# Ten early units, other store queues and other load times in the convolution tail of a two-layer image kernel

## Chip, cores and metric

The kernel runs on one core of one Trainium2 chip, in float32. The metric is the device time of one execution in microseconds (us); the median of several runs counts. The five engines are TensorE (PE), VectorE (DVE), ScalarE (ACT), GpSimd (POOL) and SyncE (SP). Each follows its own list of instructions in order; DMA transfers are issued by SP, POOL or ACT from the same lists.

## What is computed

Two layers over x of shape (2, 256, 64, 64): two images, 256 channels, 64 x 64 pixels. Layer 0 is a full attention over 4096 pixels with eight heads, blended with x by a mask. Layer 1 is a gated window attention followed by two grouped 7 x 7 convolutions, whose result gates the rows again. Cut to that:

```python
# layer 0
q = proj(Wq, bq) / sqrt(hd); k = proj(Wk, bk); v = proj(Wv, bv)
attn = softmax(einsum('bnd,bmd->bnm', q, k))            # 4096 x 4096, 16 times
hybrid = conv1x1(concat([x, attn @ v]), Wf, bf)
x = hybrid * m + x * (1 - m)
# layer 1
x = x * sigmoid(relu(x @ ca_w1 + ca_b1) @ ca_w2 + ca_b2)
x = x + window_attention(x)                             # windows of 8 x 8, four heads
x = shuffle(x)                                          # channels (4, 64) -> (64, 4)
y = relu(bn1(conv7x7(x, sa_w1, groups=64)))             # 256 -> 64 channels
y = bn2(conv7x7(y, sa_w2, groups=64))                   # 64 -> 256 channels
return x * sigmoid(y)
```

## The kernel before

**Order of the whole.** Projections come first (to about 190 us). Then a loop runs over `slots`: image b, chunk c of 512 queries, half g of the heads, block m of 128 keys. After the last block of a chunk, its denominators are computed (line 690), spread through DRAM (`inv_s`, then `rd`), and a generator `stage` (line 731) does layer 1 up to the convolutions for these 512 pixels, eight image rows. The stages of all chunks but the last run between the attention's products, a piece at a time. The stage of the last chunk of image 1 runs after the loop (lines 1227 to 1234), alternating with pieces of the convolution. Its own pieces on TensorE are, in order: hya (fuse; second half needs fa, which waits for rd), ca1, ca2, qka (twice), sca, vwa, pta, oa, opa. At its end the sum x + o is written to `xo` by VectorE (line 974) and stored to DRAM in `x_s` (line 989), in three overlapping blocks of rows. All loads of rows for the convolution read `x_s`, so those of image 1 need the last of these stores.

**The convolution.** 64 groups are taken four at a time: a unit u (16 of them, `NU`) has 16 channels. An item is a unit with image 0, with image 1 or with both; `items` (line 998) is the order in which they run. Before: units 0 to 7 of image 0, units 2 to 7 of image 1, units 8 to 15 of both, and units 1 and 0 of image 1: 24 items. Since the first eight (`EARLY`) need image 0 alone, they can run beside the last stage. For item k:

- `load_x(k)` reads its rows, 420 KB an image, into one of four buffers (`xea` for the first EARLY items, `xla` for the others, number k % 4). So the rows of item k+4 go where those of item k were.
- `load_w(u)` reads the unit's banded weights, 896 KB, into a rotating pool of eight (unit 0 has its own buffer; unit 1 is read a second time at the end).
- `conv1` (TensorE, line 1057): 28 products into one PSUM tile, of which there is one; ScalarE evicts it with Relu into `yca` (line 1065).
- `conv2` (line 1082): 56 products into two PSUM pairs; ScalarE evicts with Tanh (line 1093) and a scaling Copy (line 1099) into `z`. The trace shows each product twice.
- `gate` (line 1110): VectorE multiplies z by the rows; then 12 stores an image, 24 or 16 KB each, go to the output.

On TensorE the order is c1(k+1), c2(k), c1(k+2), c2(k+1) and so on: c1(k) and c2(k) below are conv1 and conv2 of item k. `convolve` is a generator with a yield after every conv1 and every conv2, so the gate of item k, the loads behind it and conv1 of item k+2 are written out as one piece.

**What sets the order.** The schedule is manual: each engine's list is the order in which the program writes instructions. An SP load written behind stores waits until these could be issued, and they wait for their z. Before:

- Stores alternate between POOL and SP; while `staged` is true (the last stage has ended) and k < EARLY, between POOL and ACT; for the last two items between ACT and SP. Stores on ACT are `held` and issued after the next item's evictions (line 1101).
- Behind the gate of item k the rows of item k+4 are loaded (`load_rows(k + 4)`, line 1167); at the end of the stage, four loads at once (line 1144).
- Weights: four loads ahead (units 1 to 4, line 1151), then one behind each gate: units 5 to 9 at once, units 10 and on from item 8.
- The last chunk's `x_s` stores: two on SP and two on POOL (line 988).
- Two pieces of the convolution run in the wait for the denominators (line 1230).

Of the kernel before, what the change touches and what calls it, by code (L numbers as in the profile page):

```python
# [12 lines left out]
AF = mybir.ActivationFunctionType  # L13
# [4 lines left out]
B, C, H, W = 2, 256, 64, 64  # L18
# [4 lines left out]
NCHUNK = N // CH  # L23
# [6 lines left out]
AHEAD = 2  # L30
EB = 8
DN = 8
EARLY = 8
HEADS1, HD1 = 4, 64
WS = 8
NW = W // WS
# [9 lines left out]
UG = 4  # L46
UQ = UG // 4
NU = NG // UG
# [9 lines left out]
def conv_seq_kernel(ctx: ExitStack, tc: tile.TileContext, a, out):  # L58
    nc = tc.nc
# [463 lines left out]
    def pipeline(arm, shifted, pools):  # L523
# [207 lines left out]
        def stage(b, c):  # L731
# [241 lines left out]
            for oc in range(KC):  # L973
                nc.vector.tensor_add(  # L974
                    xo[:, oc, :, PAD : PAD + W].rearrange("p r (w c) -> p w r c", c=WS),
                    y[:, oc, :].rearrange("p (w r c) -> p w r c", w=NW, r=WS),
                    u[:, oc, :].rearrange("p (w r c) -> p w r c", w=NW, r=WS),
                )
                for n, (x0, _, _) in enumerate(BLOCKS):

                    r0, r1 = max(WS * c, x0 - 1), min(WS * c + WS, x0 + 31)
                    if r0 >= r1:
                        continue
                    for h in range(2):
                        q = 2 * oc + h
                        p = 32 * q + 1 - x0

                        eng = nc.sync if h == 1 and (b, c) == (B - 1, NCHUNK - 1) else nc.gpsimd
                        eng.dma_start(  # L989
                            x_s[b, n, p + r0 : p + r1].rearrange("r g w -> g r w"),  # L990
                            xo[64 * h : 64 * h + 64, oc, r0 - WS * c : r1 - WS * c, :],
                        )
# [9 lines left out]
        def convolve():  # L1002
# [8 lines left out]
            for k in range(2):  # L1011
                t = cpool.tile([P, B * nb, WP], F32, name=f"yc{arm}{k}")
                nc.gpsimd.memset(t, 0.0)
                ycs.append(t)
            xs, ws, ys = {}, {}, {}

            weights = deque([*range(1, NU), 1])
            dst = out.rearrange("b (g i) r w -> b i r g w", i=4)
# [53 lines left out]
            def conv2(k):  # L1072
                u, images = items[k]
                n = nb * len(images)
                y = ys.pop(k)
                w = ws[u][:, 32 * UW :].rearrange("p (m d) -> p d m", d=KS)
                tiles = [psum2(f"c2{arm}{k}_{hh}") for hh in range(2)]
                for d in range(KS):
                    for j in range(4):
                        r = slice(32 * j, 32 * j + 32)  # L1080
                        for o in HALVES:
                            nc.tensor.matmul(  # L1082
                                tiles[j // 2][o, j % 2, 0 : n * W],
                                w[r, d, o],
                                y[r, 0:n, d : d + W],
                                start=(d == 0),
                                stop=(d == KS - 1),
                            )
                zs = []
                for m in range(len(images)):  # L1090
                    z = pool.tile([P, 4, nb * W], F32, tag="z", name=f"z{arm}{k}_{m}", bufs=4)
                    for hh in range(2):
                        nc.scalar.activation(  # L1093
                            z[:, 2 * hh : 2 * hh + 2, :],
                            tiles[hh][:, :, m * nb * W : (m + 1) * nb * W],
                            AF.Tanh,
                            scale=0.5,
                        )
                    nc.scalar.activation(z, z, AF.Copy, bias=0.25, scale=0.25)  # L1099
                    zs.append(z.rearrange("p j (n x) -> p j n x", x=W))  # L1100
                while held:
                    held.popleft()()
                return zs

            def gate(k, zs):
                u, images = items[k]
                for m, b in enumerate(images):
                    z = zs[m]
                    x = xs[k][:, nb * m : nb * m + nb, :, PAD : PAD + W]
                    nc.vector.tensor_mul(z, z, x.rearrange("p n g x -> p g n x"))  # L1110

                    engines = (nc.gpsimd, nc.sync)
                    if k >= len(items) - 2:
                        engines = (nc.scalar, nc.sync)
                    elif staged and k < EARLY:
                        engines = (nc.gpsimd, nc.scalar)
                    stores = 0
                    for n, (x0, r0, r1) in enumerate(BLOCKS):
                        for i in range(4):
                            p = 32 * i + 1 - x0  # L1120
                            stores += 1
                            args = (
                                dst[b, i, r0:r1, UG * u : UG * u + UG, :],
                                z[p + r0 : p + r1, :, n, :],
                            )
                            eng = engines[stores % len(engines)]
                            if eng is nc.scalar:
                                held.append(lambda a=args: nc.scalar.dma_start(*a))
                            else:
                                eng.dma_start(*args)  # L1130
                if k == len(items) - 1:
                    while held:
                        held.popleft()()


            def more():
                if staged and not xcs:

                    for n in range(3):
                        t = ep.tile([P, HG, CH], F32, tag="sum", name=f"xl{arm}{n}", bufs=3)  # L1140
                        t = t.rearrange("p h n -> p (h n)")[:, 0 : B * nb * UG * WP]
                        xcs.append(t.rearrange("p (n g w) -> p n g w", n=B * nb, g=UG, w=WP))
                    xcs.append(pool.tile([P, B * nb, UG, WP], F32, name=f"xl{arm}3"))
                    load_rows(EARLY + 3)
                return bool(xcs)


            load_rows(3)
            load_w(0)
            pool = yield  # L1150
            for _ in range(4):
                load_w(weights.popleft())
            conv1(0)
            yield
            for k, (u, images) in enumerate(items):
                while len(xs) <= k + 1 < len(items):
                    if not more():
                        yield
                conv1(k + 1)
                yield  # L1160
                more()
                z = conv2(k)
                yield
                more()
                gate(k, z)
                if xcs or k + 4 < EARLY:
                    load_rows(k + 4)

                if weights and (weights[0] <= 1 + EB or k >= EARLY):
                    load_w(weights.popleft())  # L1170

        def run_later():
# [150 lines left out]
```

## Time and profile before

| quantity | value |
|---|---|
| three runs | 2920.15, 2926.58, 2927.13 us; median 2926.58 |
| profiled execution | 2921.04 us, of it span 2919.3 us |
| mean granted TensorE clock | 0.996 |
| busy in the span | PE 2881.9, PEld 837.2, DVE 2434.9, ACT 2455.9, POOL 315.1 us |
| last attention product | ends at about 2700.6 us |
| last stage on TensorE | 2713.0 (hya) to 2763.2 us (opa) |
| conv1 and conv2 busy | 2700.2 to 2905.0 us |
| c1 products | 448 on xea, 896 on xla |
| stores of the output | 180 on POOL, 168 on SP, 36 on ACT |
| DMA in 2700 to 2920 us | 33.92 MB, mean 154 GB/s |

Times within the span count from its start. A line of the timeline gives the start, the length, engine and source line, operation, what is written and read, shape and number of instructions, and in brackets how long the engine had been idle and what ended that. PE is a matmul, PEld a weight load into the array; SPq, ACTq and POOLq are the lists that issue DMAs, and the length there is that of issuing, not of the transfer. The tail of the span, from 2700 us, is the part that the change touches.

### The profile page before, as it was taken

Reading aid. Unit: us, or ns where it says so; the run is one execution under the profiler, and the core shown is the slowest. Engines: PE = TensorE matmul, PEld = TensorE weight load, DVE = VectorE, ACT = ScalarE, POOL = GpSimd, SP = SyncE. Lnnn points to the kernel's source line nnn. Section 1 sums busy time; section 2 is a strip of 40 time slices with the busy share of each in tenths; the row PEclk is TensorE's granted clock in tenths of the full one; section 3 lists DMA queues with packets and bytes.
Section 4 is the critical chain, followed back from the end, with each engine's and each line's share of the span. In section 5 each row is a group of like instructions: output and inputs, shape, how many; then the busy total and the mean of one; then the engine's idle time right before and its main releaser. Section 6 shows DMA issues by size and latency. Waiting matters only on the chain.

```text
span 2919.3 us, 85528 instructions
## 1 busy us (share of the span) xinstructions
PE 2881.9 (99%) x37322; PEld 837.2 (29%) x37322; DVE 2434.9 (83%) x1356; ACT 2455.9 (84%) x4143; POOL 315.1 (11%) x560
## 2 busy tenths in 40 slices
PE   9999999999999999999999999999999999999998
PEld 3551222222222222222222222222222222222665
DVE  3339999899999898998989999989899899999211
ACT  5569989898989898988989898989899898989433
POOL 8010000000000101010000000000101010000356
PEclk9999999999999999999999999999999999999999
DMA  8545422222232323242222223222324232232474
GB/s 245 202 172 174 134 75 63 78 68 80 56 88 65 90 61 91 65 80 71 70 75 69 79 55 82 64 83 63 77 73 84 70 73 75 69 113 88 117 228 120
DMA packets 231124, 276.26 MB, mean 95 GB/s; under 512 B 118672, under 2 KB 135252, under 8 KB 230484
## 3 DMA queue, kind: packets, MB, share of 16 engines
q1 hardware_dynamic: 200996, 231.74, 27.3%
q0 software_dynamic: 22416, 35.61, 5.5%
q8 instruction: 295, 4.83, 0.7%
q10 hardware_dynamic: 7328, 3.36, 0.4%
q14 instruction: 89, 0.73, 0.1%
HBM read 221.88 MB, written 66.39 MB: 99 GB/s over the span
## 4 chain that ended last, share of the span: by engine, by line
PE 97%; DMA 1%; ACT 1%; DVE 0%; issue 0%; SPq 0%; POOL 0%; ACTq 0%; DVEq 0%; POOLq 0%
PE sa L633 37%; PE ava L669 35%; PE hya L519 4%; PE qka L519 4%; PE c2a L1082 2%; PE q L428 2%; PE c1a L1057 2%; PE opa L519 2%; PE vwa L519 2%; PE v L465 2%; PE k L428 2%; PE dna L695 1%; PE sca L847 1%; PE pta L922 1%; PE oa L941 1%; PE ca2a L785 1%
## 5 line engine op out<-in xcount | busy, mean ns | idle before, releaser
L646 ACT ACTIVATE ea<-sa 128x512 f32<-128x512 f32 (+1 forms) x3072 | 2036.7, 746 | 51.6 <-PE sa L633 26.6
L633 PE MATMUL sa<-qa,ka 32*64 32x512 f32 x16384 | 1145.9, 613 | 1.5 <-ACT vst L473 1.2
L675 DVE TENSOR_TENSOR suma<-suma,ea 128x2048 f32<-128x2048 f32 x480 | 1097.4, 2286 | 5.7 <-ACT ea L646 0.5
L669 PE MATMUL ava<-ea,va 128*32 128x512 f32 x8192 | 1091.1, 605 | 1.0
L675 DVE TENSOR_TENSOR odda<-odda,ea 128x2048 f32<-128x2048 f32 x420 | 959.4, 2284 | 50.6 <-ACT ea L646 50.6
L633 PEld LDWEIGHTS sa<-qa,ka 32*64 32x64 f32 x16384 | 241.7, 129 | 785.4 <-ACT ea L646 713.6
L669 PEld LDWEIGHTS ava<-ea,va 128*32 128x32 f32 x8192 | 161.5, 108 | 834.1 <-issue 804.6
L989 POOL DMA_DIRECT2D xs<-xo x94 | 66.6, 716 | 1761.8 <-DVE xo L974 1758.8
L675 DVE TENSOR_TENSOR suma<-ea,ea 128x2048 f32<-128x2048 f32 x32 | 73.2, 2287 | 58.8 <-ACT ea L646 58.8
L519 PE MATMUL qka<-ua,qkv_w 128*32 128x512 f32 x1024 | 115.8, 592 | 0.3 <-DVE ua L803 0.3
L1130 POOL DMA_DIRECT2D out_dram<-za x180 | 101.3, 571 | 77.8 <-DVE za L1110 56.3
L447 DVE TENSOR_REDUCE top<-sq 128x512 f32<-128x2048 f32 x16 | 36.6, 2286 | 81.6 <-ACT sq L441 81.6
L750 ACT ACTIVATE ta<-hya,bf 128x512 f32<-128x512 f32 x32 | 20.2, 683 | 97.3 <-PE hya L519 91.3
L1110 DVE TENSOR_TENSOR za<-za,xla 128x768 f32<-128x768 f32 x24 | 23.0, 960 | 94.3 <-ACT za L1099 53.7
L707 POOL DMA_DIRECT2D invs<-inva x62 | 34.1, 558 | 599.2 <-DVE inva L721 438.9
L754 DVE TENSOR_TENSOR ta<-ta,mca 128x512 f32<-128x512 f32 x32 | 22.0, 688 | 77.4 <-ACT ta L750 77.4
L868 ACT ACTIVATE ewa<-ewa,mxwa 128x64 f32<-128x64 f32 x256 | 85.3, 346 | 1.5 <-DVE mxwa L859 1.5
L1082 PE MATMUL c2a<-yca,wa 32*64 32x192 f32 (+1 forms) x2688 | 83.7, 387 | 2.6 <-issue 2.3
L1093 ACT ACTIVATE za<-c2a 128x384 f32<-128x384 f32 x64 | 27.8, 486 | 57.9 <-PE c2a L1082 41.6
L826 ACT ACTIVATE qka<-qka,qkv_b 128x512 f32<-128x512 f32 x64 | 40.3, 681 | 40.8 <-PE qka L519 40.8
L1082 PEld LDWEIGHTS c2a<-yca,wa 32*64 32x64 f32 x2688 | 64.7, 192 | 22.0 <-issue 12.7
L677 DVE TENSOR_TENSOR suma<-suma,odda 128x2048 f32<-128x2048 f32 x30 | 68.8, 2292 | 1.0
(138 smaller groups left out, 1675.9 us busy)
## 6 DMA issues: line engine op xcount, KB each, us to landing
ka<-ks SPq DMA_DIRECT2D x256, 256.0 KB
va<-vs SPq DMA_DIRECT2D x256, 256.0 KB
wa<-ws SPq DMA_DIRECT2D x17, 896.0 KB
ws<-zeros SPq DMA_DIRECT2D x16, 896.0 KB
xs<-xo POOLq DMA_DIRECT2D x78, 140.0 KB, 6.0
xla<-xs SPq DMA_DIRECT2D x24, 420.0 KB
x<-in_x_dram SPq DMA_DIRECT2D x16, 512.0 KB
qs<-qst SPq DMA_DIRECT2D x16, 512.0 KB
```

What stands on the lines that cost most here:

```text
L428: nc.tensor.matmul(s[:, g, :], w[:, kc, g * P : (g + 1) * P], rhs, start=(kc == 0), stop=(kc == KC - 1),)
L465: nc.tensor.matmul(sv[:, m, :], xs0[i][:, kc, m * P : (m + 1) * P], wv[:, kc, :], start=(kc == 0), stop=(kc == KC - 1),)
L519: nc.tensor.matmul(out[o : o + 32], weights[:, o : o + 32], x, start=start, stop=stop)
L633: nc.tensor.matmul(heads[j][o], k[r, cols][:, o], q[r, g, :], start=True, stop=not shifted)
L646: nc.scalar.activation(e[:, h, :], tile, AF.Exp, scale=SCALE0)
L669: nc.tensor.matmul(av[r, :], v[:, m % PB, r], e[:, j, :], start=start, stop=stop)
L675: nc.vector.tensor_add(total, first.pop(m % chains, total), e)
L677: nc.vector.tensor_add(acc[1], acc[1], acc[2])
L868: nc.scalar.activation(e[:, n, :], e[:, n, :], AF.Exp, bias=mx[:, n : n + 1], accum_out=rs[:, n : n + 1],)
L989: eng.dma_start(x_s[b, n, p + r0 : p + r1].rearrange("r g w -> g r w"), xo[64 * h : 64 * h + 64, oc, r0 - WS * c : r1 - WS * c, :],)
L1082: nc.tensor.matmul(tiles[j // 2][o, j % 2, 0 : n * W], w[r, d, o], y[r, 0:n, d : d + W], start=(d == 0), stop=(d == KS - 1),)
L1130: eng.dma_start(*args)
```

## The change

- `EARLY` is 10: units 0 to 9 of image 0 run by themselves, then units 2 to 9 of image 1, units 10 to 15 of both, and units 1 and 0 of image 1: 26 items.
- Stores of an item go to POOL alone until `staged`, then to POOL and SP in turn. Nothing is held on ACT but half the stores of the last item.
- The last item's z is evicted, gated and stored by blocks of 64 columns (three of them) instead of whole.
- All four `x_s` stores of the last chunk go to SP.
- Two weight loads go ahead instead of four. Behind the gate of item k, unit u is loaded once `due(u)` is at most k: units 3 and 4 behind item 1, units 5 to 9 behind items 2 to 6, units 10 to 15 behind items 15 to 20, unit 1 again behind item 21.
- Rows of items below EARLY are loaded behind item k-4 as before; those of the others, k+3 behind item k's stores, one item at a time, and not four at once.
- One more piece of the convolution, c2(1), runs ahead of the last stage's hya.

The order that results on TensorE around the last stage is: c1(0), c1(1), denominators, c2(0), c1(2), c2(1), hya, c1(3), ca1, ca2, c2(2), qka, c1(4), sca, qka, c2(3), sca, vwa, c1(5), pta, c2(4), oa, c1(6), opa, c2(5), c1(7), c2(6), c1(8). Before it was: c1(0), c1(1), denominators, c2(0), c1(2), hya, c2(1), ca1, ca2, c1(3), qka, c2(2), sca, qka, c1(4), sca, vwa, c2(3), pta, c1(5), oa, c2(4), opa, c1(6), c2(5), c1(7), c2(6), c1(8).

```diff
-EARLY = 8
+EARLY = 10
...
-                        eng = nc.sync if h == 1 and (b, c) == (B - 1, NCHUNK - 1) else nc.gpsimd
+                        eng = nc.gpsimd
+                        if (b, c) == (B - 1, NCHUNK - 1):
+                            eng = nc.sync
...
+            at_unit = [0]
...
+                    if k < len(items) - 1:
+                        evict(z, tiles, slice(m * nb * W, (m + 1) * nb * W))
                     zs.append(z.rearrange("p j (n x) -> p j n x", x=W))
-                while held:
-                    held.popleft()()
-                return zs
+                return zs, tiles
...
+            def store(k, b, n, z, engines):
+                u = items[k][0]
+                x0, r0, r1 = BLOCKS[n]
+                for i in range(4):
+                    p = 32 * i + 1 - x0
+                    eng = engines[(4 * n + i) % len(engines)]
...
+            def gate(k, zs, tiles):
+                for m, b in enumerate(items[k][1]):
...
+                    if k == len(items) - 1:
+                        for n in range(nb):
+                            evict(z[:, :, n, :], tiles, slice(n * W, (n + 1) * W))
+                            nc.vector.tensor_mul(z[:, :, n, :], z[:, :, n, :], x[:, :, n, :])
+                            store(k, b, n, z, (nc.sync, nc.scalar))
+                        while held:
+                            held.popleft()()
+                        continue
+                    nc.vector.tensor_mul(z, z, x)
+                    engines = (nc.gpsimd,)
+                    if staged:
+                        engines = (nc.gpsimd, nc.sync)
+                    for n in range(nb):
+                        store(k, b, n, z, engines)
...
+            def due(u):
+                if u < EARLY:
+                    return max(1, u - 3) if len(ws) < NU else len(items) - 5
+                return u + EARLY - 5
...
-                    load_rows(EARLY + 3)
+                if xcs:
+                    load_rows(min(len(xs), at_unit[0] + 2))
                 return bool(xcs)
...
-            for _ in range(4):
+            for _ in range(2):
                 load_w(weights.popleft())
...
-                gate(k, z)
-                if xcs or k + 4 < EARLY:
+                gate(k, *z)
+                at_unit[0] = k + 1
+                if k + 4 < EARLY:
                     load_rows(k + 4)
-
-                if weights and (weights[0] <= 1 + EB or k >= EARLY):
+                more()
+
+                while weights and due(weights[0]) <= k:
                     load_w(weights.popleft())
...
-            if now[0] in (len(slots) + DN, len(slots) + DN + 1):
+            if len(slots) + DN <= now[0] <= len(slots) + DN + 2:
                 next(conv)
```

More of the change, by code (lines that the diff above doesn't have):

```diff
@@ L1091, in conv2 @@
                     z = pool.tile([P, 4, nb * W], F32, tag="z", name=f"z{arm}{k}_{m}", bufs=4)
[L1092 to L1099, printed above, removed]
@@ L1100, in conv2 @@
-                    zs.append(z.rearrange("p j (n x) -> p j n x", x=W))
-                while held:
-                    held.popleft()()
-                return zs
-            def gate(k, zs):
-                u, images = items[k]
-                for m, b in enumerate(images):
+                    if k < len(items) - 1:
+                        evict(z, tiles, slice(m * nb * W, (m + 1) * nb * W))
+                    zs.append(z.rearrange("p j (n x) -> p j n x", x=W))
+                return zs, tiles
@@ new lines, in evict @@
+            def evict(z, tiles, cols):
+                for hh in range(2):
+                    nc.scalar.activation(
+                        z[:, 2 * hh : 2 * hh + 2, :],
+                        tiles[hh][:, :, cols],
+                        AF.Tanh,
+                        scale=0.5,
+                    )
+                nc.scalar.activation(z, z, AF.Copy, bias=0.25, scale=0.25)
+            def store(k, b, n, z, engines):
[4 more added lines that the diff above has]
+                    eng = engines[(4 * n + i) % len(engines)]
+                    args = (
+                        dst[b, i, r0:r1, UG * u : UG * u + UG, :],
+                        z[p + r0 : p + r1, :, n, :],
+                    )
+                    if eng is nc.scalar:
+                        held.append(lambda a=args: nc.scalar.dma_start(*a))
+                    else:
+                        eng.dma_start(*args)
@@ L1108, in gate @@
+            def gate(k, zs, tiles):
+                for m, b in enumerate(items[k][1]):
                     z = zs[m]
                     x = xs[k][:, nb * m : nb * m + nb, :, PAD : PAD + W]
[L1110 to L1130, printed above, removed]
@@ L1131, in gate @@
-                if k == len(items) - 1:
-                    while held:
-                        held.popleft()()
+                    x = x.rearrange("p n g x -> p g n x")
+                    if k == len(items) - 1:
[6 more added lines that the diff above has]
+                        continue
```

## The prediction

> **What bounds the kernel now.** I read the share of the chain by engine, then the timeline behind the last attention product, the granted clock by microsecond, and the queue of SyncE. An item is a unit of 16 channels for one image or for both; c1(k) and c2(k) are the two convolutions of item k on TensorE, and e(k) is the end of c2(k).
>
> ```profile
> PE 97%; DMA 1%; ACT 1%; DVE 0%; issue 0%; SPq 0%; POOL 0%; ACTq 0%; DVEq 0%; POOLq 0%
> ```
>
> The chain is TensorE nearly throughout. The diff leaves everything before 2700 us alone, so only the last 219 us of the span can move, and there it matters when TensorE waits. The timeline just after the last stage (its last projection ends at 2762.9, counted to the modelled end of its work):
>
> ```profile
> 2764.65 1.39 SPq L989 DMA_DIRECT2D xs<-xo  x2
> ...
> 2769.01 11.08 ACTq L1128 DMA_DIRECT2D out_dram<-za  x6
> ...
> 2772.76 2.90 SPq L1036 DMA_DIRECT2D xla<-xs  x4
> 2772.76 3.76 PE L1082 MATMUL c2a<-yca,wa 32*64 32x192 f32 x107 [1.73 <-issue]
> ...
> 2780.14 0.42 ACT L1065 ACTIVATE yca<-c1a,cbias 128x192 f32<-128x192 f32 x1 [10.34 <-DMA xla<-xs]
> ...
> 2780.61 4.26 PE L1057 MATMUL c1a<-xla,wa 128*32 128x192 f32 x56 [4.09 <-ACT yca L1065]
> ```
>
> Here TensorE runs dry: image 1 must be stored and read back, and six held stores sit on ScalarE's queue for 11.08 us ahead of the eviction that c1(8) needs. Idle 1.73 + 4.09 us; two convolutions also run slowly, 3.76 and 4.26 us. Why, the stretches of 1 us show (columns: length, PE, PEld, DVE, ACT, POOL, granted clock, DMA share, GB/s):
>
> ```profile
> 2773.00:2774.00 1.00, 1.00 (x57) 1.00 (x57) 0.00 (x0) 0.00 (x0) 1.00 (x3) 1.00 0.31 43
> 2774.00:2775.00 1.00, 1.00 (x42) 1.00 (x35) 0.00 (x0) 0.00 (x0) 1.00 (x3) 0.51 0.78 226
> ...
> 2783.00:2784.00 1.00, 1.00 (x20) 0.62 (x16) 0.19 (x1) 0.00 (x0) 0.51 (x1) 0.50 0.04 7
> 2784.00:2785.00 1.00, 1.00 (x28) 0.55 (x27) 0.00 (x0) 0.00 (x0) 1.00 (x3) 0.87 0.34 73
> ```
>
> The granted clock halves at 2774.0, although TensorE is busy again and had idled only 1.73 us, and comes back at 2784.2. Beyond that TensorE is dense. One item there:
>
> ```profile
> 2789.83 2.64 PE L1082 MATMUL c2a<-yca,wa 32*64 32x192 f32 x112
> ...
> 2794.26 0.96 DVE L1110 TENSOR_TENSOR za<-za,xla 128x768 f32<-128x768 f32 x1 [4.07 <-ACT za L1099]
> ...
> 2795.24 2.54 SPq L1130 DMA_DIRECT2D out_dram<-za  x6
> ...
> 2797.45 2.53 PE L1057 MATMUL c1a<-xla,wa 128*32 128x192 f32 x56
> ...
> 2797.90 0.39 SPq L1036 DMA_DIRECT2D xla<-xs  x1
> ```
>
> c2(8) ends at 2792.47. Its gate ends at 2795.22, its six SyncE stores are issued by 2797.78, and only then, 5.43 us after e(8), goes the load of rows: those of item 12, whose c1 starts at 2802.48. The next two items give 5.29 and 5.33; I take 5.35. Between lies c1(11), at 2797.45, before the load is issued.
>
> **The work itself.** Convolution steps start 2.47 (c1) and 2.57 us (c2) apart for one image, 4.73 and 4.80 for two: 5.04 and 9.53 an item. Splitting units 8 and 9 costs 2 x (10.08 - 9.53) = +1.1. By the changed order c1(6) moves ahead of the last projection, -2.5 behind it; c2(1) in turn fills the 1.68 us in which TensorE waits for fa, and the stage after it swaps equals (c1 for c2), so I put no change there. Unhindered, after the projection: 7.61 (c2(5), c1(7), c2(6)) + 10.08 (to e(8)) + 110.15 (c1(10) to c2(25)) = 127.84 us, ending at 2890.7. Now it ends at 2905.0: **-14.3**, the gain of filling the gap with image 0.
>
> **The stage: weights of unit 3 come late.** Four weight loads go out ahead now, two afterwards:
>
> ```profile
> 2688.37 7.49 SPq L1029 DMA_DIRECT2D wa<-ws  x4
> ...
> 2756.00 0.39 SPq L1036 DMA_DIRECT2D xea<-xs  x1
> 2756.44 0.48 SPq L1029 DMA_DIRECT2D wa<-ws  x1
> ```
>
> Units 3 and 4 follow only behind the gate of item 1 and the rows of item 5, which reuse its buffer. In the changed order VectorE does that gate after the last x1 addition, and c1(3) stands on TensorE right behind the second half of hya, ahead of ca1:
>
> ```profile
> 2718.33 3.64 PE L519 MATMUL hya<-fa,WfT 128*32 128x512 f32 x32 [1.68 <-DVE fa L727]
> ...
> 2722.04 1.26 ACT L750 ACTIVATE ta<-hya,bf 128x512 f32<-128x512 f32 x2 [8.33 <-PE hya L519]
> ...
> 2724.81 0.69 DVE L756 TENSOR_TENSOR x1a<-ta,xa 128x512 f32<-128x512 f32 x1
> ```
>
> From the end of hya (2721.97) x1 is done after 3.53, the gate after 0.95 more, then rows and weights: for such a pair (2756.00 and 2756.44) DMA traffic starts 1.2 us after the first issue and reaches zero at 2762.0; landing, I estimate, 6.2 after that issue (between 5.5 and 7.0). So c1(3) waits 3.53 + 0.95 + 6.2 = 10.7 us, and behind it ca1, ca2, the gating, the projections: the stage itself. Then c1(3) 2.47, ca1 1.28, and 4.44 from its end to qka as now: 18.9 from hya to qka, where now it is 8.67, so +10.2, and some 2 more for the halved clock after such a gap: **+12** (9 to 14). Cover: none; the two convolutions that filled these gaps are the ones that wait.
>
> **Unit 8's weights.** All four last xs stores now stand on SyncE (two did), 0.70 us each, ahead of item 5's stores, the rows of item 9 and w8. In the changed program each SyncE DMA waits for the landing of the eighth before it: the rows wait for the third xs store, issued 1.7 + 1.4 after the projection and landing 5.8 later (the page's POOL rows of such stores say 5.8 and 6.0), and w8 lands 6.2 behind that: 15.1, with rounding 15.2, against c1(8) due at 7.6: **+7.6** (5.6 to 9.1).
>
> **Rows three ahead.** The load behind item k's stores now serves item k+3, due one item after e(k), 5.04 later, but issued 5.35 after e(k). A load of two images (2870.37) has traffic from 1.2 to 4.2 us; one image I take at 1.2 + 1.3 + 0.9 = 3.4 to land (from 2.6, data only, to 4.6, what c1(14) saw in full traffic). So 5.35 + 3.4 - 5.04 = 3.7 late; that wait gives the next item its time, so every second one pays: items 10, 12, 14, 16: **+14.8** (11.6 to 20.0). Item 18 has two images and weights w10 in the same place: 5.35 + 7.3 - 5.04 = **+7.6** (6.7 to 8.9; 7.3 = 6.2 plus another 0.43 MB at the 330 to 390 GB/s of these loads). Two-image items put 12 stores first: 8.0 to 9.5 us from e(k) to the load, I take 8.7, then 7.3, against 9.53 plus whatever the item before waited: items 20 to 25 pay 3.1, 2.2, 3.1, 2.2, 2.0, 1.6 = **+14.2** (13.2 to 19.3).
>
> **The clock.** By the row at 2774.0 a wait of 1.7 us in a stretch of 3.4 is enough to halve the clock for the next stretch, which costs up to 1.7 of busy time; 11 of these waits are longer: 11 x 1.2 = **+13.2** (0 to 18).
> [...]
>
> **What costs nothing.** GpSimd takes all 12 stores of an item in the stage, 12 x 0.57 = 6.8 us, where items come some 9 us apart; rda is ahead of them in its queue. Were items nearer than 6.8, the z buffers (four) would hold the evictions. ScalarE is rid of 36 issues; the 11.08 us one was under the read-back of image 1, whose 5.8 + 6 us decided anyway. **The end**: now 14.3 us from c2's end to the span's; afterwards the last item is evicted in three blocks, 3.4 to the last gate, 2.5 for six held stores, 2.5 to land, and 3.4 as now from the last byte (2915.9) to the end: 11.8, **-2.5**.
>
> **Sum**: -14.3 - 2.5 + 12 + 7.6 + 14.8 + 7.6 + 14.2 + 13.2 = +52.6. The profiled execution took 2921.04 (span 2919.3), 5.5 under the median of the three runs, 2926.58 (2920.15 to 2927.13). 2921.0 + 52.6 = **2974**. With all low bounds +29 (2950), with all high ones +72 (2993).
>
> **Rivals.** (a) *The fill wins* (faster): loads land as early as their items need them. Then -14.3 - 2.5, **2904**. Point: all waits and slow clock together below 16.8 us. For it: DMA share about 0.5 when weights are spread. Against: 5.35 to the issue alone exceeds 5.04. 4 in 100. (b) *Only the start is late*, rows being hidden: -16.8 + 12 + 7.6 + 2.4 clock = +5, **2926**, about no change. It needs rows to land in -0.3 us. 6 in 100. (c) *Unit 3 is not late*, because its load slips in earlier: +52.6 - 12, **2962**. Against: the queue order. 15 in 100. (d) *Waits reinforce each other*, POOL's stores holding z: above **2993**; 10 in 100. The forecast: 65 in 100.
>
> A measurement of this kernel tells about 0.3% (9 us) from no change. Range 2940 to 3000, which holds (c) and most of (d). Faster 0.04, within 0.3% 0.05, slower 0.91.
>
> **What would show it.** c1 of item 3 waiting some 10 us on w right behind hya; c1(8) some 8; then every second c1 with a wait of 3 to 5 on xla, the clock at 0.5 in parts; no ACTq rows until the end; c2's last end near 2960. Wrong, if c1(10) to c1(16) follow at 5.04, or if the weights' landing takes much less than 5 us.

## The result, and the profile after

The changed kernel takes 2989.01 us (median of four runs, 2985.88 to 2992.84); the kernel before, on the same chip, 2925.26 (2920.15 to 2927.13). The ratio is 1.0221, interval 1.0203 to 1.024. The profiled execution took 2985.88 us, span 2984.0 against 2919.3: 64.7 us more. The forecast was 2974 (2940 to 3000); it was counted from the profiled execution, and from profile to profile the loss is 64.8 us where 52.6 were forecast.

A yardstick for all that follows is the *stretch* from the start of the first conv1 to the end of the last conv2 in the profile. What lies before it differs by up to 9 us between executions and chips (2699.6 us in run 5, 2708.6 in run 7), whatever the kernel does later. Before: 2700.25 to 2905.0, 204.8 us. After: 2701.46 to 2971.0, 269.6 us. So the whole loss lies in the stretch; 1.2 us come from ahead of it, and the end behind it is 1.3 shorter (13.0 against 14.3).

What TensorE waited for in it, in the view of waits (total us, times, longest). First the kernel before:

```profile
PE c1a L1057 <- ACT yca L1065: 4.7, 2, 4.1
PE c2a L1082 <- issue: 2.3, 2, 1.7
PE hya L519 <- DVE fa L727: 1.7, 1, 1.7
PE c1a L1057 <- DMA out_dram<-za: 1.2, 1, 1.2
```

And after:

```profile
PE c1a L1060 <- DMA wa<-ws: 34.4, 7, 11.4
PE c1a L1060 <- DMA xla<-xs: 16.4, 4, 4.5
PE c1a L1060 <- issue: 8.5, 2, 7.7
```

The three waits that the change was able to remove (1.7 for fa, 1.7 and 4.1 in the gap behind the stage) are gone. In their place conv1 waits 59.3 us in these three lines, and the releasers are loads: weights 34.4, rows 16.4. (The 8.5 of "issue" are one wait of 7.73, which run 3 shows to be for a load, and a stall of 0.80, which is not.) The timeline of TensorE shows where:

```profile
2720.38 3.62 PE L519 MATMUL hya<-fa,WfT 128*32 128x512 f32 x32
2735.44 4.51 PE L1060 MATMUL c1a<-xea,wa 128*32 128x192 f32 x56 [11.44 <-DMA wa<-ws]
...
2792.14 4.72 PE L1060 MATMUL c1a<-xea,wa 128*32 128x192 f32 x56 [7.73 <-issue]
...
2808.56 3.81 PE L1060 MATMUL c1a<-xla,wa 128*32 128x192 f32 x56 [3.75 <-DMA xla<-xs]
2812.30 2.63 PE L1085 MATMUL c2a<-yca,wa 32*64 32x192 f32 x112
2814.86 2.54 PE L1060 MATMUL c1a<-xla,wa 128*32 128x192 f32 x56
...
2824.48 4.20 PE L1060 MATMUL c1a<-xla,wa 128*32 128x192 f32 x56 [4.51 <-DMA xla<-xs]
...
2877.24 7.56 PE L1060 MATMUL c1a<-xla,wa 128*32 128x384 f32 x56 [7.63 <-DMA wa<-ws]
```

c1(3) stands right behind hya and waits 11.44 us for the weights of unit 3, and the last stage waits with it. c1(8) waits 7.73. Then the pattern of three ahead: c1(10) waits 3.75 for its rows, c1(11) follows at once, c1(12) waits 4.51, and so on. Item 18, the first with both images, waits 7.63. Each conv1 behind a wait of 3.7 us or more is slow: 3.81 to 4.72 us instead of 2.54 for one image, 6.13 to 7.56 instead of 4.81 for two.

Why c1(3) waits is on SyncE's queue and VectorE:

```profile
2715.00 13.84 SPq L1039 DMA_DIRECT2D xea<-xs  x2
2728.94 0.91 SPq L1032 DMA_DIRECT2D wa<-ws  x2
```

```profile
2727.45 0.95 DVE L1138 TENSOR_TENSOR za<-za,xea 128x768 f32<-128x768 f32 x1
```

The load of rows ahead of the weights needs the buffer that the gate of item 1 reads; that gate ends at 2728.40. The weights of units 3 and 4 are issued from 2728.94, and c1(3) starts 6.5 us later.

The rows of item 10, for which c1(10) waits, go behind the stores of item 7:

```profile
2802.55 2.47 SPq L1123 DMA_DIRECT2D out_dram<-za  x6
2805.19 0.39 SPq L1039 DMA_DIRECT2D xla<-xs  x1
```

That is 5.42 us after the end of c2(7) (2799.77), and c1(10) starts 3.37 us later.

The stretches of 10 us tell how much of the time TensorE lost, and that DMA was not what ran out (columns: length, PE, PEld, DVE, ACT, POOL, granted clock, DMA share, GB/s):

```profile
2730.00:2740.00 10.00, 4.56 (x64) 3.25 (x68) 0.00 (x0) 0.00 (x0) 5.77 (x11) 0.52 0.72 251
...
2820.00:2830.00 10.00, 5.52 (x120) 4.81 (x128) 0.96 (x1) 2.12 (x4) 4.73 (x9) 0.83 0.51 130
2830.00:2840.00 10.00, 6.28 (x232) 5.49 (x216) 1.92 (x2) 3.86 (x7) 4.05 (x8) 0.93 0.30 75
```

In the items of image 1 TensorE is busy for little over half of these slices and the DMA engines for 30 to 51%: the transfers are not too many, they are issued too late. Runs 2 and 4 test that.

### The profile page after: what moved, and what is told of

The parts are those of the page before. It is cut to its first block, busy times and chain, and to the rows that moved or that the text cites. A ratio compares the mean times of both kernels' runs of the same rounds, so it can differ in the third digit from the quotient of the medians.

```text
span 2984.0 us, 86218 instructions
## 1 busy us (share of the span) xinstructions
PE 2899.4 (97%) x37658; PEld 850.4 (28%) x37658; DVE 2436.2 (82%) x1358; ACT 2457.7 (82%) x4151; POOL 333.9 (11%) x594
## 4 chain that ended last, share of the span: by engine, by line
PE 94%; DMA 2%; ACT 1%; SPq 1%; DVE 1%; issue 1%; POOL 0%; ACTq 0%
PE sa L633 36%; PE ava L669 34%; PE qka L519 4%; PE hya L519 4%; PE c1a L1060 2%; PE opa L519 2%; PE v L465 2%; PE vwa L519 2%; PE q L428 2%; PE c2a L1085 2%; PE k L428 1%; DMA wa<-ws 1%; PE dna L695 1%; SPq L1123 1%; PE sca L847 1%; PE ca2a L785 1%
## 5 line engine op out<-in xcount | busy, mean ns | idle before, releaser
L1123 POOL DMA_DIRECT2D out_dram<-za x216 | 121.3, 569 | 136.5 <-DVE za L1138 115.6
L1060 PE MATMUL c1a<-xla,wa 128*32 128x192 f32 (+1 forms) x896 | 69.3, 472 | 39.2 <-DMA wa<-ws 22.7
L1068 ACT ACTIVATE yca<-c1a,cbias 128x192 f32<-128x192 f32 (+1 forms) x26 | 12.0, 460 | 107.4 <-PE c1a L1060 107.4
L1102 ACT ACTIVATE za<-c2a 128x384 f32<-128x384 f32 (+1 forms) x68 | 28.3, 467 | 63.0 <-PE c2a L1085 54.6
```

The costliest lines, as they stand in the source:

```text
L1060: nc.tensor.matmul(s[32 * j : 32 * j + 32, 0 : n * W], w[:, j, d, :], xs[k][:, 0:n, j, d : d + W], start=(d == 0), stop=(d == KS - 1),)
```

## The experiments

Twelve kernels. "Stretch" is as defined above, from the one profiled execution of each. The first four ran on one chip (kernel before there: 2924.32), the next four on a second (2929.28), the last four on a third (2926.19); "the fourth run" in the expectations is the one with everything loaded earlier.

| run | time, us | ratio to before, interval | stretch, us |
|---|---|---|---|
| before, profiled | 2921.04 | | 204.8 |
| the change | 2989.01 | 1.0221 [1.0203, 1.024] | 269.6 |
| 1 four weights ahead | 2977.35, one run | | 263.6 |
| 2 rows four ahead | 2962.82, one run | | 247.5 |
| 3 early weights one item earlier | 2982.84, one run | | 266.3 |
| 4 all loads earlier | 2915.92 | 0.9969 [0.9958, 0.998] | 200.0 |
| 5 waits filled, 30 matmuls | 2996.34 | 1.0231 [1.0205, 1.0258] | 275.8 |
| 6 all earlier, eight units | 2956.67 | 1.0098 [1.0082, 1.0115] | 236.6 |
| 7 all earlier, late weights at u+1 | 2925.95 | 0.9982 [0.9972, 0.9992] | 206.0 |
| 8 all earlier, stores on SyncE too | 2928.1 | 0.9997 [0.9988, 1.0007] | 202.1 |
| 9 waits filled, 16 matmuls | 2978.72 | 1.0177 [1.0157, 1.0198] | 263.1 |
| 10 eight units, late weights at u+1 | 2917.42 | 0.9968 [0.9954, 0.9982] | 202.6 |
| 11 late weights alone earlier | 2976.81 | 1.0171 [1.015, 1.0191] | 264.0 |
| 12 the change, stores on SyncE too | 3002.33 | 1.0258 [1.024, 1.0275] | 280.1 |

### 1. Four weights ahead, as before

```diff
-            for _ in range(2):
+            for _ in range(4):
                 load_w(weights.popleft())
```

> The changed kernel with four weight loads ahead instead of two (units 3 and 4 are no longer behind the gate of item 1). Theory (unit 3's weights hold the last stage): c1(3) follows hya with no wait, the 11.4 us wait and the 2.0 us of slow clock behind it go, opa ends some 13 us earlier, the whole is 2976 (from 2989); the waits of items 8, 10, 12, 14, 16 and 18 stay as they are. Rival (the later waits absorb it, since they are bound to something else): the stage ends earlier but the end moves less than 4 us, 2985 or more.

Measured: 2977.35 us. TensorE's timeline of this run:

```profile
2718.93 3.62 PE L519 MATMUL hya<-fa,WfT 128*32 128x512 f32 x32
2722.36 2.49 PE L1060 MATMUL c1a<-xea,wa 128*32 128x192 f32 x56
```

c1(3) follows hya without a wait, 2.49 us long. That settles the first term: the wait of 11.44 was the two weight loads taken from the front. The time is 11.7 us under the change's median and 8.5 under its profiled execution; in the stretch only 6.0 us are saved, less than half of the 13.4 that the wait and its slow clock cost: of the later waits, those of items 10, 12 and 14 grow from 3.75, 4.51 and 4.19 to 4.85, 4.83 and 4.72, with conv1 at 4.7 each time, and c1(20) and c1(22) wait longer too (4.06 and 6.15 against 3.70 and 5.12). Why they grow isn't shown. For item 10 SyncE's rows name a part: the six stores ahead of its rows took 3.45 us instead of 2.47, and the load went out 6.42 us after the end of c2(7) instead of 5.42.

### 2. Rows four items ahead

```diff
-                    load_rows(min(len(xs), at_unit[0] + 2))
+                    load_rows(min(len(xs), at_unit[0] + 3))
```

> The changed kernel with rows loaded four items ahead instead of three (all else as changed). Theory (the load behind the stores comes after its convolution is due): the waits of c1(10), c1(12), c1(14), c1(16) on rows, 16.4 us together, and about 7.9 us of slow clock in them go; item 18 still waits some 7 us for its weights and the later two-image items for theirs; 2965. Rival (the landing is limited by DMA traffic, not by the place in the queue): waits of 2 us or more stay at these items and the gain is at most 8 us, 2981.

Measured: 2962.82 us, stretch 22.1 shorter: the largest single part. The same items in the timeline:

```profile
2803.99 2.55 PE L1060 MATMUL c1a<-xla,wa 128*32 128x192 f32 x56
...
2814.60 2.55 PE L1060 MATMUL c1a<-xla,wa 128*32 128x192 f32 x56 [0.44 <-DMA xla<-xs]
...
2855.24 7.12 PE L1060 MATMUL c1a<-xla,wa 128*32 128x384 f32 x56 [9.92 <-DMA xla<-xs]
```

At items 10 to 16 nothing is left but 0.44 us. c1(18) now waits 9.92 instead of 7.63. The view names rows, but its own rows went out 13.7 us before it starts; the weights of unit 10 went out 7.3 before it, 7.65 us after the end of c2(15) (6.30 in the change), behind the rows of item 19. The prediction had it that a load issued 5.35 us after its item's end cannot serve an item that starts 5.04 after it; one item more of lead is enough.

### 3. The first weights one item earlier

```diff
-                    return max(1, u - 3) if len(ws) < NU else len(items) - 5
+                    return max(1, u - 4) if len(ws) < NU else len(items) - 5
```

> The changed kernel with units 5 to 9 loaded one item earlier (w8 ahead of the last chunk's stores to DRAM on SyncE, w9 behind item 5). Theory (distance and queue place make w8 late): the 7.7 us wait of c1(8) and about 2.5 us of slow clock go, c1(9) waits up to 3 us instead; 2981 (2978 to 2985). Rival (c1(8) waits for something else, since the profile names no DMA there): the wait stays, 2989.

Measured: 2982.84 us.

```profile
2784.80 2.77 PE L1060 MATMUL c1a<-xea,wa 128*32 128x192 f32 x56
...
2792.53 2.54 PE L1060 MATMUL c1a<-xea,wa 128*32 128x192 f32 x56 [2.16 <-DMA wa<-ws]
```

c1(8), the first line, no longer waits; c1(9) then waits 2.16 for its weights and c1(10) 2.75 for its rows: part of what was gained is a smaller wait a little later, and the stretch is only 3.3 shorter. It also names the 7.73 us that the view put down to "issue": they go when the weights are issued an item earlier, so they were a wait for w8.

### 4. All loads earlier

```diff
-                    return max(1, u - 3) if len(ws) < NU else len(items) - 5
-                return u + EARLY - 5
+                    return max(0, u - 5) if len(ws) < NU else len(items) - 7
+                return u + 3
...
-                    load_rows(min(len(xs), at_unit[0] + 2))
+                    load_rows(min(len(xs), at_unit[0] + 3))
...
-            for _ in range(2):
+            for _ in range(4):
```

> The changed kernel with all loads put ahead: four weights ahead, units 5 to 9 behind items 0 to 4, units 10 to 15 behind items 13 to 18, unit 1 behind item 19, rows four items ahead. Theory (all that the change lost is lateness of loads, and the fill with image 0 is worth 14 us): no wait of c1 above 1.5 us, TensorE's last convolution ends near 2891 to 2895, time 2906 to 2912, that is faster than before (2925). Rival (DMA traffic takes the place of lateness where weights and one-image items meet, items 13 to 17): waits of 2 us and more there, 2918 or more.

Measured: 2915.92 us (eight runs), ratio 0.9969 [0.9958, 0.998]: 73 us below the change and 0.3% faster than the kernel before, but 4 to 10 above what was expected, and so between the theory (2912 at most) and the rival (2918 or more). Its waits:

```profile
PE c1a L1060 <- issue: 4.1, 2, 2.8
PE c1a L1060 <- ACT yca L1068: 0.6, 1, 0.6
...
PE c1a L1060 <- DMA xla<-xs: 0.2, 1, 0.2
```

Of 58.5 us of waits for loads 0.2 are left. So the other parts of the change (ten units, the store queues, the evictions by blocks), taken together, cost nothing of the 63.8: it was the time of the loads. Runs 1, 2, 3 and 11, each of which moves one group of loads, save 6.0 + 22.1 + 3.3 + 5.6 = 37.0 us of the stretch, all together 69.6. By the change's median they save 11.7 + 26.2 + 6.2 + 12.2 = 56.3 of 73.1. Run 3 moved its group by one item and run 4 by two, so this isn't quite the same edit in parts; but a quarter to a half shows only when nothing else is late.

What keeps it from 2912 is seen in its timeline, in the middle of c1(17), and in the stretches of 1 us there (columns as above):

```profile
2819.52 1.88 PE L1060 MATMUL c1a<-xla,wa 128*32 128x192 f32 x40
2824.24 1.32 PE L1060 MATMUL c1a<-xla,wa 128*32 128x192 f32 x16 [2.84 <-issue]
2825.49 3.79 PE L1085 MATMUL c2a<-yca,wa 32*64 32x192 f32 x112
```

```profile
2823.00:2824.00 1.00, 0.00 (x0) 0.00 (x0) 0.00 (x0) 0.00 (x0) 0.80 (x2) 1.00 0.90 237
2824.00:2825.00 1.00, 0.76 (x14) 0.59 (x16) 0.00 (x0) 0.00 (x0) 0.79 (x2) 0.79 0.96 289
2825.00:2826.00 1.00, 1.00 (x24) 0.47 (x24) 0.00 (x0) 0.39 (x1) 1.00 (x3) 0.50 0.97 238
```

Forty records (20 of the 28 products) run, so the rows and weights of this item are there; then TensorE stands for 2.84 us, while the DMA engines are mostly 90% busy or more with later weights, rows and stores; and conv2 behind it takes 3.79 at a granted clock of 0.50. The stall stands where the rival put one (items 13 to 17), but it is no wait for rows or weights; the view names nothing that TensorE waited for, only "issue".

### 5 and 9. Are the slow convolutions the clock?

In the change every wait of 3.7 us or more has a slow conv1 behind it (3.81 to 7.56 us). To part the two, TensorE is given work in the wait:

```diff
             def conv1(k):
...
+                if k in (10, 12, 14, 16):
+                    idle = avp.tile([P, CH], F32, tag="av", name=f"idle{arm}{k}")
+                    some = wf.rearrange("p k o -> p (k o)")[:, 0:CH]
+                    for i in range(30):
+                        r = slice(32 * (i % 4), 32 * (i % 4) + 32)
+                        nc.tensor.matmul(idle[r, :], ones[:, 0:32], some, start=True, stop=True)
```

> The changed kernel with 30 matmuls 32x512 on constant data, whose result nobody reads, ahead of the first convolutions of items 10, 12, 14 and 16: they fill the waits for rows (3.75, 4.51, 4.19 and 3.99 us) with TensorE work and need some 0.11 us each, 3 to 3.5 us, so the rows are waited for no longer than before. Theory (the slow first convolutions behind those waits, 3.81 to 4.72 us against 2.54, are the granted clock, which fell because TensorE stood idle): the granted clock stays at 1.0 in those four places, the four convolutions take 2.5 to 2.7 us, and 5 to 7 us are saved: 2981 to 2984 us against 2989. Rival (they are slow for another reason that comes with the wait, such as data arriving in parts): they still take 3.8 to 4.7 us, 2988 to 2990.

Measured: 2996.34 us. Both numbers were missed for one reason: each of these products is recorded twice, as all here, and 30 took 6.63 us instead of 3.3, more than the wait. But the conv1 behind them were not slow: 52 of the 56 records took 2.46 us at items 10, 12 and 16, 54 of them 2.87 at item 14. Run 9 has 16 instead of 30:

> The changed kernel with 16 instead of 30 matmuls of constant data ahead of the first convolutions of items 10, 12, 14 and 16. In the run with 30 they took 6.63 us, two records of 0.11 us each, more than the waits they were to fill; 16 take some 3.5 us, less than the waits of 3.75 to 4.51 us. Theory (the slow first convolutions behind those waits are the granted clock): the four take 2.5 to 2.7 us instead of 3.81, 4.20, 4.72 and 4.71, the waits that are left are 0.3 to 1 us, and the time is 6 to 7 us below the changed kernel's, 2982 to 2984 us beside a kernel before of 2925. Rival (the convolutions are slow because the rows arrive in parts): no change, 2988 to 2990.

Measured: 2978.72 us, stretch 6.5 shorter, as the theory said (the time fell by 10 against the change's median, more than expected, and by 7.3 against its profiled execution). Its timeline and a slice:

```profile
2816.55 3.64 PE L1062 MATMUL idlea<-WfT,ones 128*32 128x512 f32 x32
2820.98 2.54 PE L1066 MATMUL c1a<-xla,wa 128*32 128x192 f32 x56 [0.79 <-DMA xla<-xs]
```

```profile
2820.00:2830.00 10.00, 9.21 (x297) 8.27 (x301) 0.96 (x1) 2.56 (x5) 3.90 (x8) 1.00 0.34 84
```

The rows come as late as in the change, 0.79 us of wait are left, and conv1 takes 2.54: with the granted clock at 1.00 where it was 0.83. So the slow convolutions are the clock, which falls because TensorE idles, and not rows that arrive in parts. Useless work made the kernel faster than the change.

### 6 and 10. Are ten units needed?

Run 6 is run 4 with `EARLY = 8`.

> Everything loaded earlier as in the fourth run, but eight units of image 0 by themselves instead of ten. Theory (with the loads in time the two additional units are what fills the stretch in which TensorE waited for the last stage before): without them TensorE stands idle some 10 to 14 us longer around 2720 to 2770, and the time is 2925 to 2930 us against 2915.9. Rival (the gain of the fourth run comes from loading alone, the two units fill nothing that is needed): 2913 to 2918.

Measured: 2956.67 us, 27 above the theory's upper end. The edit was not the single step that it was meant to be: with eight units, unit u + 3 is three items ahead of the late units, where it is five with ten. TensorE waited 19.9 us for weights at the two-image items. Run 10 puts that right:

```diff
-EARLY = 10
+EARLY = 8
...
-                return u + 3
+                return u + 1
```

> Eight units of image 0 by themselves and everything loaded early, the late weights now at unit + 1, which is five items ahead as in the fourth run with ten units (the run with eight units before had them at unit + 3, three items ahead, and waited 19.9 us for them). Theory (the two additional units cover the time until the rows of image 1 are there, some 10 us, and nothing else): a wait of 6 us for the first rows of image 1 and a slow convolution of 1.9 us behind it remain, and 0 to 4 us of smaller waits; 8 to 12 us above the fourth run: 2924 to 2929 us, about the kernel before. Rival 1 (the two units are not needed): 2914 to 2919. Rival 2 (eight units with early loads wait at each two-image item whatever the weights do): 2940 or more.

Measured: 2917.42 us, ratio 0.9968 [0.9954, 0.9982]. Rival 1 is right on the time: from ten units (0.9969) it can't be told apart. The theory is right on the place:

```profile
2775.70 4.71 PE L1060 MATMUL c1a<-xla,wa 128*32 128x192 f32 x56 [4.80 <-DMA xla<-xs]
```

With eight units conv1 of the first item of image 1 waits 4.80 us for its rows and then takes 4.71; with ten that 7 us is covered. But in the stretch ten units are only 2.6 better. They cost 1.1 by themselves (two units split by image), and in run 4 stood the stall of 2.84 and its slow conv2 (1.15). Whether that stall belongs to the ten units or to where the loads fell is open; one execution each can't say. Runs 6 and 10, which differ in one number, also give the price of late weights when the other loads, but for the first rows of image 1, are in time: 34.0 us of stretch for two items of lead. In run 11 the same two items are worth 5.6.

### 7. Late weights two items earlier still

```diff
-                return u + 3
+                return u + 1
```

> Everything loaded earlier as in the fourth run, and the weights of units 10 to 15 two items earlier still (due at unit + 1 instead of unit + 3). Theory (the 2.84 us that TensorE stood in the middle of the first convolution of item 17, and the lower clock behind it, come from weights and two-image rows that share the DMA engines at 2820 to 2850): the load is spread, the stall and the slow convolution go, 2910 to 2913 us. Rival (the crowding only moves to the items of image 1): 2914 to 2919, with a stall of the same kind elsewhere.

Measured: 2925.95 us, stretch 206.0. The theory is wrong: the stall in c1(17) is gone, but c1(18) waits 3.29 us for its rows and takes 6.12, and eight "issue" stalls of 0.3 to 1.5 stand elsewhere, where run 4 had three. The stalls moved, as the rival said, and cost more; that crowding of the DMA engines makes them is not shown. Some 9 us of the profiled execution lie ahead of the stretch, for which I have no cause.

### 8 and 12. The stores

Run 12 is the change, run 8 is run 4, both with the stores on GpSimd and SyncE from the first item on:

```diff
-                    engines = (nc.gpsimd,)
-                    if staged:
-                        engines = (nc.gpsimd, nc.sync)
+                    engines = (nc.gpsimd, nc.sync)
```

> The changed kernel with stores by GpSimd and SyncE from the first item on: the part 'stores by GpSimd until the last stage ends' undone, all else as changed. Theory (the loads are issued too late to bear anything ahead of them on SyncE's queue): the six stores of item 1, some 0.5 us each, stand ahead of the weights of unit 3, whose wait grows from 11.4 to some 14 to 15 us, and those ahead of other loads cost up to 5 us more: 2992 to 2998 us against 2989. Rival (the stores slip into idle time of the queue): 2987 to 2991.

Measured: 3002.33 us, 13.3 above the change and 4 above the theory's upper end. SyncE's queue there:

```profile
2729.68 2.45 SPq L1123 DMA_DIRECT2D out_dram<-za  x6
2732.23 0.39 SPq L1039 DMA_DIRECT2D xea<-xs  x1
2732.67 0.97 SPq L1032 DMA_DIRECT2D wa<-ws  x2
```

Six stores of item 1 stand ahead of w3 for 2.45 us; c1(3) waits 13.29 (+1.9), c1(6), which had waited 0.24, 3.83 for its weights, c1(8) 8.12. So the stores by GpSimd alone are a good part of the change: given loads this late they save 10.6 us of the stretch. The end behind the stretch is longer too, 18.2 instead of 13.0.

> Everything loaded earlier as in the fourth run, but the stores by GpSimd and SyncE from the first item on, so that the part 'stores by GpSimd alone until the last stage ends' is undone. Theory (that part matters only where a load is due right behind a store on SyncE's queue; with rows and weights loaded far ahead nothing is): 2914 to 2919 us, no change. Rival (SyncE's waits for the store data hold the loads back again): waits of the first convolutions for rows or weights of over 2 us each in the first ten items, 2922 or more.

Measured: 2928.1 us, ratio 0.9997 [0.9988, 1.0007]; against run 4's 0.9969 that is some 8 us more, and the theory (no change) is wrong on the time. Its mechanism isn't the rival's either: no conv1 of the first ten items waits for rows or weights; c1(18) waits 2.25 for rows, c1(6) stands 2.05 on "issue", and the rest of it takes 4.01 us instead of 2.35. The stretch is 2.1 us longer, the end behind it 18.5 us instead of 12.4. So 6 of the 8 us lie in the end, which is longer in run 12 as well (18.2). In run 8 the DMA engines move at most 11 GB/s in the last 7.7 us, in the change 8 GB/s in the last 2, in run 4 at most 16 in the last 3. What makes the end longer is not settled.

### 11. The late weights alone

```diff
-                    return max(1, u - 3) if len(ws) < NU else len(items) - 5
-                return u + EARLY - 5
+                    return max(1, u - 3) if len(ws) < NU else len(items) - 7
+                return u + EARLY - 7
```

> The changed kernel with the weights of units 10 to 15, and the one that is loaded a second time, due two items earlier, rows and first weights as in the change. Theory (from item 18 on it is the weights that come last): the waits for weights at 18 (7.63 us) and 20 to 24 (15.1 us) and the 6 us of slow convolutions behind them shrink, but the rows of two images, still three ahead, come next and leave 2 to 3 us at each of 18, 20, 22 and 24: 13 to 20 us saved, 2969 to 2976. Rival 1 (the rows are as late as the weights): less than 6 us saved, 2983 or more. Rival 2 (the weights are all of it): 27 to 30 us saved, 2959 to 2962.

Measured: 2976.81 us (two runs, 2975.1 and 2978.52), 12 below the change by the medians, just short of the theory's 13, but only 5.6 by the stretch, as rival 1 had it. Its waits:

```profile
PE c1a L1060 <- DMA xla<-xs: 28.3, 7, 5.7
PE c1a L1060 <- DMA wa<-ws: 11.4, 2, 11.2
```

and item 18 in its timeline:

```profile
2879.11 6.62 PE L1060 MATMUL c1a<-xla,wa 128*32 128x384 f32 x56 [5.73 <-DMA xla<-xs]
```

The waits for weights fall from 34.4 to 11.4, and what is left is c1(3). But those for rows rise from 16.4 to 28.3, and 6.7 us of waits for evictions are new. At item 18 the rows are waited for 5.73 us, where it was 7.63 for the weights: the rows were only 1.9 us less late, and moving the weights uncovers them. The waits for rows at items 10 to 16, ahead of the loads that were moved, are 2.5 us longer too, for which no cause is shown.

## Why the prediction was right, step by step

The mechanism was right: the waits came where it named them, for the loads it named, but at items 23 and 25, which did not wait. The time, 2989, lies in the range, 15 us above the forecast; 12 of them are loss beyond the sum, 3 that the median lies above the profiled execution. One term was sized by a wrong step, the clock. By the terms, predicted against the profile after:

| term | predicted | measured | from |
|---|---|---|---|
| fill of the gap by image 0 | -14.3 | -12.5 | not seen by itself: the stretch's 64.8 less the terms below the end's |
| the end | -2.5 | -1.3 | 13.0 against 14.3 |
| the stage waits for w3 | +12 | +12.4 | opa ends 13.6 later, less 1.2 from ahead |
| c1(8) waits for w8 | +7.6 | +7.7 | 7.73 |
| rows at 10, 12, 14, 16 | +14.8 | +16.4 | 3.75 + 4.51 + 4.19 + 3.99 |
| item 18 | +7.6 | +7.6 | 7.63 |
| items 20 to 25 | +14.2 | +15.1 | 3.70 + 1.18 + 5.12 + 5.11, none at 23 and 25 |
| slow clock | +13.2 | +18.1 | each conv above its usual time, but c1(3), which is in the stage's term |
| sum | +52.6 | +63.5 | the first row is a remainder, so it closes by itself; with the 1.2 from ahead of the stretch, the span's 64.7 |

- **The clock** was the term that was mis-sized. I took 1.2 us for each of eleven waits from one row of the trace before, and "0 to 18" for the whole. Nine waits of 3.7 us or more were followed by a slow conv1, by 1.3 to 2.75 us, 1.92 on average (2.0 with the conv2 behind it); the wait of 1.18 at item 21 by none. The 18.1 lie just above the 18 that I gave as the most. The step that failed is the price of one wait, not the mechanism: I let a wait halve the clock for one stretch of 3.4 us, a length that no row of the kernel before shows by itself. At items 10, 12, 20 and 22 the clock was at 0.50 for 3.41 us, and they cost 1.3 to 1.7; at items 8, 14, 16, 18 and 24 for 6.83 or 10.24, and they cost 2.2 to 2.75. Run 9 showed that the slow convolutions go when TensorE is kept busy, rows as late as before.
- **The stage** (12 against 12.4) and **w8** (7.6 against 7.7) were each shown by moving that load alone (runs 1 and 3). The 12.4 hold 0.9 us by which c2(1) is longer than the wait it fills, which I had put at nothing. The stage's order, worked out from x1, gate, rows, weights, is what SyncE's and VectorE's rows show.
- **Rows three ahead**: 1.6 us more than predicted, in the range (11.6 to 20.0). Run 2 shows that it is the lead and not the amount of data: the same bytes, one item earlier, leave 0.44 us.
- **Items 18 to 25**: the sums were right (7.6; 15.1 against 14.2), the places not all: 3.1, 2.2, 3.1, 2.2, 2.0, 1.6 were predicted, and the waits fell mainly on every second item instead (3.70, 1.18, 5.12, none, 5.11, none), as at 10 to 16.
- **The end**: I gave the last six stores on ScalarE 2.5 us; they took 5.26.

```profile
2974.85 5.26 ACTq L1121 DMA_DIRECT2D out_dram<-za  x6
```

- **The gain of the fill**: by the balance of the change 12.5 of the predicted 14.3 is there. With all loads in time less of it remains: the stretch is only 4.8 shorter than before (200.0 against 204.8), since the stall in c1(17), smaller ones and the slow clock behind them take 6 to 8 us back, by their sum in the timeline.
- **Rivals.** (a), the fill wins, fell here, and came true only in run 4, 12 us above its 2904. (b), rows hidden, fell by c1(10) to c1(16). (c), unit 3 not late, fell by c1(3), and run 1 measured what it would have been worth: 11.7 us by the median, 6.0 of the stretch, where 12 were said. (d), waits that reinforce each other, is closer to the opposite: one wait hides another, as run 11 shows at item 18, and as the parts that don't add up to run 4 suggest.

## What to carry to other kernels

A load behind the work of one item, for an item n later, has n items minus the queue ahead of it to land: work out issue and landing against the use for each kind of load, since one step of lead here was worth 22 us and DMA share (0.3 to 0.5) gave no hint. Where several loads are late together, one can hide another, so judge them by moving all of them; single repairs gave 37.0 us of 69.6 in the stretch. And price a wait on TensorE with the slow clock behind it: about 2 us here for each wait of 3.7 us or more.

## What the runs showed of the hardware

- The granted clock fell to 0.50 after idle times of 1.73 us (before) and 2.84 us (run 4). Behind every wait of 3.2 us or more that the runs' timelines show for conv1, it was slow: 3.81 to 4.72 us for one image, where 2.54 is usual, and 6.07 to 7.56 for two, where 4.81 is. It kept its usual time behind waits of 1.07 (run 9), 1.18 (the change), 2.02 (run 11), 2.16 (run 3) and 2.25 us (run 8), but not behind 2.26 us (run 11: 3.69 instead of 2.54). So the length of a wait alone doesn't decide. The price did not follow the wait either: conv1 for one image took 4.71 behind 3.99 us, 4.20 behind 4.51 and 4.72 behind 7.73.
- From 2700 us on the granted clock of the change was at 0.50 eleven times: for 3.41 us four times, for 6.83 three times, for 10.24 three times, and from 2975.12 to the end. In the 3.41 us ahead of each of these TensorE was busy for 0 to 1.11 us, in the kernel before for 1.28 and 1.68 us ahead of its two. In the 3.43 us ahead of the end of the wait for fa (1.68 us, before) it was busy for 1.75, and the clock stayed at 1.00. Which waits are followed by such a spell, and what sets its length, is not shown.
- TensorE stopped within a group of equal products, whose first records had run, so that rows and weights were there; the view names nothing that it waited for ("issue"). In c1(6) it stood each time behind the first six records: for 0.80 us in the change, 1.24 in run 4, 1.50 in run 7 and 2.05 in run 8; in c1(17) of run 4, behind forty, for 2.84. What these stalls are is not shown.
- Run 4 shows the other side of loading early: with the DMA engines 83 to 91% busy from 2820 to 2850 no load is late, but TensorE's longest stall falls there.
